# Own values first, keys and queries later, and expert tails beside the causal attention's units

## The chip, the cores and the metric

The kernel runs on one core of one Trainium2 chip, which is called trn2 below. The metric is the device time of one execution in microseconds (us). The times given are the median of three runs, with the lowest and the highest; the profile is of one execution of its own, whose time stands beside it.

## The reference

2048 tokens of width 128 go through a chain of layers, each added to the stream `x`. The first layers (a feed-forward, an attention, a feed-forward, and a mixture of experts on either side of a long convolution) are not touched. What follows is:

```python
# L2: half a feed-forward, rotary attention over all tokens, half a feed-forward
x = x + 0.5 * swiglu(norm(x))
x = x + attention(rope(norm(x) @ Wq), rope(norm(x) @ Wk), norm(x) @ Wv) @ Wo   # 16 heads of 8
x = x + 0.5 * swiglu(norm(x))
# then twice a gated block, with a causal rotary attention between the two
def gated_block(x):
    rows = norm(x)
    q = rows @ q_w;  q = q * 2 * sigmoid(head_scale(q))
    ctx = attention(q, rows @ k_w, rows @ v_w)          # all tokens, 16 heads of 8
    rows = rows + (sigmoid(ctx @ gate_w + gate_b) * ctx) @ out_w
    rows = norm(rows) * n1_g + n1_b
    out = rows + weight * (rows + res_scale * expert(rows))   # one of 8 experts for each token, by the router
    return x + 0.5 * (norm(out) * n2_g + n2_b)
x = gated_block(x)
x = x + causal_attention(rope(...)) @ Wo                # L3: as L2's, with a causal mask
x = gated_block(x)
```

(This is cut and written in short; the widths, the norms and the order are those of the reference.) All of it is float32.

## The kernel before, in words

**Tiles and units.** The tokens are cut into four chunks (`NC` = 4) of 512 (`CW`), each of four tiles of 128 (`TC` = 4). The 16 heads form four groups (`NG`) of four. A unit of an attention is (query chunk, group). For each unit two passes are made: a score pass (`sn` on TensorE, and `h_mx` on VectorE for the maximum of each row), and a weight pass (`st` on TensorE, `pr` = exp on ScalarE, `av` on TensorE). Between the passes the maxima are transposed (`mt_ps`), cast (`h_mT`) and written as extra rows into the query tile by four small DMAs (`qp<-h_mT`). At the end of a unit it is normalised (`close`), and after the fourth group of a chunk the projection is added to the stream (`finish`).

**The loop.** `attend` runs steps n = 0, 1, 2, and so on. A step takes one weight piece of the unit under way and one score piece of the unit that comes one or two later, each in two halves, so that TensorE, VectorE and ScalarE overlap. While no weights have been computed the mode is "fill"; then it is "core"; and once the scores of this call are done, the scores of the next call (`after`) begin, in mode "drain". What runs outside of the loops has mode "free", and "host" is the mode of the earlier mixture of experts, which has chunk tasks of the first call as its guests. The attention calls are, in order: `rope2` (L2), `gated[0]`, `rope3` (L3, causal), `gated[1]`.

**Guests.** Chunk tasks are Python generators, and each `yield` gives the number of ticks after which the task goes on. The list `beside` holds the chains of tasks; `guests()` advances the first two of it, twice for each step in "fill" and once elsewhere. Among them are `prepare(c)` (norm, transpose, keys of chunk c, and for chunk 0 its query), `value(c)` (the values into `va`), `query(c)`, `l2_chunk(c)` (half a feed-forward) and `route(c)` (the router). `carried` is what the previous call has left over. At L1135, L1136 and L1137 it is set that the carried chains come first, then the chunk's own values, and that `asking` holds the queries of chunks 1 to 3, which start as soon as the first unit is scored.

**Order on the engines.** Instructions of the loop are pinned: each engine keeps the order in which the program issues them. TensorE is in order, so an instruction that waits holds up all that stands behind it. The loads have their queues: most are issued by SyncE (`SP`), the rotary tables (`cos`, `sin`, L883) by GpSimd (`POOL`) outside of "free".

**Keys and queries.** In "fill" the keys of a chunk are spread on the chip (`keys_here`, L793): projection `pj`, rotation `rot`, then for each group two `spread` products and two evictions into `kp`. In the other modes `send` writes them to DRAM (`dk`), and `load_keys` reads them back into `kp`, half by half, in four loads of 128 KB for each half; where they wait in `waiting_keys`, the next call issues these loads at its beginning. Queries go to DRAM too (`dq`), and `begin` reads a unit's back into a `qp` tile.

**Rows of ones.** `head_buffers` has a function `rows`, which fills `qp`, the extra rows of `kp` (in whole columns of 128 partitions) and `va` at the start of the first call: half 0 on VectorE and ScalarE, half 1 later on GpSimd. L1564, L1572, L1576 and L1579 are these fills.

**Norms.** `norm` (L196) takes statistics on VectorE, then an inverse square root in small instructions (L185 to L188), which are on GpSimd in the modes "host" and "fill" and otherwise on VectorE, and normalises on ScalarE (L213).

**Experts.** `Experts.run` (L1325) computes the products for the slots of the experts, and then gathers each chunk's results by indirect DMAs (L1500) into `yg`. `tail(c)` weights and adds them, norms the sum and adds it to the stream. After `experts[0]`, the tails and `rope3.prepare(c)` of chunks 0 to 2 are run to their end one after another, outside of a loop, and the fourth chunk's go as a carried chain into the causal call:

```python
            for c in range(NC - 1):
                finish_all([tail(c), *after(c)])
            return [chain([tail(NC - 1), *after(NC - 1)])]
```

Of the kernel before, what the change touches and what calls it, by code (L numbers as in the profile page):

```python
# [21 lines left out]
P = 128  # L22
# [8 lines left out]
HD = 8  # L31
# [12 lines left out]
def tile_macaron(ctx: ExitStack, tc: tile.TileContext, a: dict, out: bass.AP):  # L44
# [151 lines left out]
    def norm(src, dst, on_act=False):  # L196
        stats = small.tile([P, TC, 6], F32, tag="ln_stats", name="ln_stats")
        mv = small.tile([P, TC, 2], F32, tag="ln_mv", name="ln_mv")
        for t in range(TC):
            vec.bn_stats(stats[:, t, :], src[:, t, :])  # L200
            vec.bn_aggr(mv[:, t, :], stats[:, t, :])
        on_pool = on_act and order["mode"] in ("host", "fill")
        rstd = inv_sqrt(small, mv[:, :, 1], [P, TC], "ln", on_pool)
# [514 lines left out]
    def four(ps):  # L718
        return ps.rearrange("p (t d) -> p t d", d=D)
# [48 lines left out]
    class Heads:  # L768
# [23 lines left out]
        def keys_here(self, c):  # L792
# [3 lines left out]
            for g in (0, 1, 3, PARK):  # L796
# [8 lines left out]
                self.loaded.add((c, g))  # L805
                yield 1

        def send(self, which, c):
# [9 lines left out]
            if which == "q":  # L818
                self.sent.add(c)
            elif order["mode"] == "drain":  # L820
                self.load_keys(c, (0,))
                self.waiting_keys.append((c, (1,)))
            else:
                self.waiting_keys.append((c, (0, 1)))
# [34 lines left out]

        def query(self, c):  # L860
            yield from self.send("q", c)

# [9 lines left out]
    class RopeHeads(Heads):  # L872
# [18 lines left out]
        def project(self, which, c, hi, lo):  # L891
            tables = list(self.tables(c))
            cols = self.wp[self.pre + "_bcol"]
            n = 0 if which == "q" else 2
# [83 lines left out]
    def attend(A, carried, follow, after=None):  # L978
# [156 lines left out]
        own = chain([A.value(c) for c in range(NC)])  # L1135
        asking = [chain([A.query(c) for c in range(1, NC)])]  # L1136
        beside += [[0, task] for task in (*carried[len(beside):], own)]  # L1137
        followed = 0
# [14 lines left out]
        while nw < len(weights) or last:  # L1153
# [14 lines left out]
            if s and B is not A and units[0] not in B.queries:  # L1168
                if 0 in B.sent:
                    begin(B, units[0])  # L1170
                else:
                    s = None
            if s and s[1] not in B.queries:
                s = None
# [67 lines left out]
    class Experts:  # L1242
# [82 lines left out]
        def run(self, carried, after):  # L1325
# [170 lines left out]
            for c in range(NC):  # L1496
                results.append(four(wide_tile("yg")[:, 0:CW]))
                for t in range(TC):
                    i = c * TC + t
                    nc.gpsimd.indirect_dma_start(  # L1500
                        results[c][:, t, :], None, og[:, :],
                        bass.IndirectOffsetOnAxis(ap=slot_i[:, i : i + 1], axis=0),
                    )

            def tail(c):
                yg = results[c]
                y = self.heads.rows[c]
                for t in range(TC):
# [3 lines left out]
                    )  # L1512
                norm(y, y, on_act=True)
                vec.tensor_tensor(y, y, bc(w["b3_n2g"], TC), ALU.mult)
                vec.tensor_tensor(tiles_of(x, c), tiles_of(x, c), y, ALU.add)
                yield 2

            for c in range(NC - 1):
                finish_all([tail(c), *after(c)])
            return [chain([tail(NC - 1), *after(NC - 1)])]  # L1520

# [32 lines left out]
    def head_buffers(pool):  # L1554
# [6 lines left out]
        def rows(half):  # L1561
# [6 lines left out]
            for p in range(4 * half, 4 * half + 4):  # L1568
                dst = kp[:, p, 0:n].rearrange("p (t d) -> p t d", d=P)
                src = ones.unsqueeze(1).to_broadcast([P, n // P, P])  # L1570
                if p < 2:
                    nc.scalar.activation(dst, src, AF.Identity, bias=one_rows, scale=0.0)  # L1572
                else:
                    engine = nc.gpsimd if half else nc.vector
                    tc.keep_in_program_order(
                        engine.tensor_scalar(dst, src, 0.0, one_rows, ALU.mult, ALU.add)  # L1576
                    )
            if half == 0:
                tc.keep_in_program_order(nc.gpsimd.memset(va_flat, 1.0))  # L1579

# [44 lines left out]
    carried = attend(gated[0], carried, lambda c: [experts[0].route(c)])  # L1625
    carried = experts[0].run(carried, lambda c: [rope3.prepare(c)])
    carried = attend(rope3, carried, lambda c: [gated[1].prepare(c)], gated[1])
# [110 lines left out]
```

## Time and profile before

| what | value |
| --- | --- |
| median of 3 runs | 4072.75 us (4072.22 to 4075.01) |
| profiled execution | 4067.55 us, span 4065.8 us |
| granted TensorE clock over the span | 0.886 |
| TensorE busy | 3587.3 us (88%) |
| VectorE busy | 3124.2 us (77%) |
| ScalarE busy | 2377.6 us (58%) |
| GpSimd busy | 293.5 us (7%) |

The stages, by the times of their first and last instructions in the trace (us from the start of the span): the layers up to the experts of L1 to 742, with the first chunk tasks of L2 as guests from 490; `rope2` 742 to 1557; `gated[0]` to 2370; the experts' products to 2486, with gathers from 2488; tails and keys of three chunks to 2556; `rope3` to 3124; `gated[1]` to 3905; the second experts, tails and store to 4066.

How to read it: PE is TensorE, PEld its weight loads, DVE VectorE, ACT ScalarE, POOL GpSimd, SP SyncE, and a q behind the name means its queue. The page has the span in 40 slices of 101.6 us with the busy tenths of each engine and the granted clock (PEclk). The table of windows gives the busy time of each engine in a stretch, with the number of instructions. The chain of waits follows the work that ended last back from step to step; its pieces named "issue" are time in which the engine waited for nothing that the profile shows. A mean over the span mixes stages with different limits.

### The profile page before, as it was taken

Reading aid. Unit: us, or ns where it says so; the run is one execution under the profiler, and the core shown is the slowest. Engines: PE = TensorE matmul, PEld = TensorE weight load, DVE = VectorE, ACT = ScalarE, POOL = GpSimd, SP = SyncE. Lnnn points to the kernel's source line nnn. Section 1 sums busy time; section 2 is a strip of 40 time slices with the busy share of each in tenths; the row PEclk is TensorE's granted clock in tenths of the full one; section 3 lists DMA queues with packets and bytes.
Section 4 is the critical chain, followed back from the end, with each engine's and each line's share of the span. In section 5 each row is a group of like instructions: output and inputs, shape, how many; then the busy total and the mean of one; then the engine's idle time right before and its main releaser. Section 6 shows DMA issues by size and latency. Waiting matters only on the chain.

```text
span 4065.8 us, 72224 instructions
## 1 busy us (share of the span) xinstructions
PE 3587.3 (88%) x29160; PEld 1706.7 (42%) x29160; DVE 3124.2 (77%) x5433; ACT 2377.6 (58%) x4513; POOL 293.5 (7%) x557
## 2 busy tenths in 40 slices
PE   8779899689999996899999965689997899999965
PEld 8656655333333343333333343343333333333333
DVE  2855344569999984799999844699996799999844
ACT  1222133158888873688888722256675588888732
POOL 2100011220000000000000023200000000000013
PEclk8889799879999997899999966588898799999965
DMA  2100001120000002100000022400002100000012
GB/s 65 31 1 1 1 8 34 45 61 7 10 8 8 7 2 53 35 7 10 7 10 5 7 62 78 109 15 10 10 2 63 40 9 7 10 7 7 7 51 66
DMA packets 63695, 98.97 MB, mean 24 GB/s; under 512 B 9104, under 2 KB 29312, under 8 KB 63104
## 3 DMA queue, kind: packets, MB, share of 16 engines
q1 hardware_dynamic: 53200, 69.22, 6.2%
q0 software_dynamic: 8816, 24.55, 2.5%
q8 instruction: 230, 3.77, 0.4%
q14 instruction: 105, 0.86, 0.1%
q10 hardware_dynamic: 1344, 0.57, 0.1%
HBM read 64.25 MB, written 29.00 MB: 23 GB/s over the span
## 4 chain that ended last, share of the span: by engine, by line
PE 76%; DVE 12%; ACT 4%; issue 3%; POOL 2%; DMA 2%; SPq 0%; POOLq 0%; ACTq 0%; DVEq 0%
PE av L76 23%; PE st L76 18%; PE sn L1006 10%; PE po L76 5%; PE h L76 5%; DVE h_mx L84 4%; ACT pr L1063 2%; PE ph L76 2%; DVE st L84 1%; PE km L76 1%; PE gu L76 1%; PE ot_ps L94 1%; PE mt_ps L94 1%; PE kv L76 1%; DVE ln_stats L84 1%
## 5 line engine op out<-in xcount | busy, mean ns | idle before, releaser
L84 DVE TENSOR_REDUCE h_mx<-sn 128x2 f32<-128x1024 f32 (+1 forms) x1856 | 2206.1, 1197 | 142.4 <-PE sn L1006 120.0
L1063 ACT ACTIVATE pr<-st 128x512 f32<-128x512 f32 x3712 | 1972.8, 585 | 510.5 <-PE st L76 331.7
L76 PE MATMUL av<-pr,va 128*32 128x256 f32 x14592 | 1187.1, 397 | 11.1 <-ACT h_ot L1092 11.1
L76 PE MATMUL st<-qp,kp 64*128 64x512 f32 x3712 | 998.2, 499 | 48.2 <-ACT pr L1063 45.9
L1006 PE MATMUL sn<-kp,qp 64*128 64x512 f32 (+3 forms) x3712 | 811.8, 415 | 122.0 <-DVE h_mx L84 49.0
L76 PEld LDWEIGHTS st<-qp,kp 64*128 64x128 f32 x3712 | 393.7, 187 | 821.5 <-ACT pr L1063 442.4
L76 PEld LDWEIGHTS av<-pr,va 128*32 128x32 f32 x14592 | 292.6, 109 | 663.1 <-issue 625.8
L1006 PEld LDWEIGHTS sn<-kp,qp 64*128 64x128 f32 x3712 | 387.5, 195 | 177.0 <-issue 64.2
L614 ACT ACTIVATE hid<-h 128x512 f32<-128x512 f32 x128 | 76.3, 597 | 232.5 <-PE h L76 226.9
L84 DVE TENSOR_TENSOR hid<-hid,h 128x512 f32<-128x512 f32 x128 | 87.3, 687 | 112.6 <-PE h L76 100.6
L76 PEld LDWEIGHTS po<-w_l_w3T,hid 128*128 128x128 f32 x1024 | 126.6, 194 | 39.0 <-issue 27.7
L76 PE MATMUL po<-w_l_w3T,hid 128*128 128x128 f32 x1024 | 128.7, 278 | 5.4 <-DVE hid L84 5.3
L1420 POOL DMA_INDIRECT wt<-in_b_wt,w_row_i x30 | 28.7, 958 | 1429.1 <-DVE slot_i L84 1384.5
L76 PE MATMUL h<-m_xc,w_l_w12T 128*128 128x512 f32 x256 | 126.8, 633 | 0.1
L76 PE MATMUL h<-xnT,w_l_w12T 128*128 128x512 f32 x256 | 117.4, 601 | 0.4 <-DVE logits L594 0.4
L247 POOL TENSOR_TENSOR x<-x,w_b_n2b 128x512 f32<-128x512 f32 x8 | 10.1, 1265 | 1126.3 <-DVE rows L84 1121.0
L84 DVE BATCH_NORM_STATS2 st<-ph 128x6 f32<-128x256 f32 x46 | 19.9, 432 | 89.7 <-PE ph L76 89.7
L1035 ACT CAST h_mT<-mt_ps 8x512 fp32r<-8x512 f32 x64 | 36.9, 576 | 67.9 <-PE mt_ps L94 67.7
L84 DVE TENSOR_TENSOR st<-st,mask_kq 128x128 f32<-128x128 f32 x256 | 63.2, 290 | 14.1 <-PE st L76 13.3
L76 PEld LDWEIGHTS h<-m_xc,w_l_w12T 128*128 128x128 f32 x256 | 49.6, 204 | 50.6 <-issue 47.3
L213 ACT ACTIVATE xn_t<-x,ln_nb,ln_r 128x128 f32<-128x128 f32 x52 | 21.4, 482 | 79.7 <-POOL ln_nb L208 67.9
L94 PE MATMUL xn_tp<-ident,xn_t 128*128 128x128 f32 x64 | 20.8, 406 | 52.6 <-ACT xn_t L213 49.1
(422 smaller groups left out, 2923.7 us busy)
## 6 DMA issues: line engine op xcount, KB each, us to landing
qp<-dq SPq DMA_DIRECT2D x128, 136.0 KB
kp<-dk SPq DMA_DIRECT2D x76, 128.0 KB
dq<-hi SPq DMA_DIRECT2D x32, 256.0 KB
dq<-lo SPq DMA_DIRECT2D x32, 256.0 KB
wt<-in_b_wt SPq DMA_DIRECT2D x16, 258.0 KB
qp<-h_mT SPq DMA_DIRECT2D x240, 4.0 KB
cos<-in_l_cos POOLq DMA_DIRECT2D x12, 256.0 KB, 4.1
sin<-in_l_sin POOLq DMA_DIRECT2D x12, 256.0 KB, 5.2
```

The costliest lines, as they stand in the source:

```text
L76: pin(nc.tensor.matmul(dst, lhsT=lhsT, rhs=rhs, start=start, stop=stop))
L84: ins = method(*args, **kw)
L94: pin(nc.tensor.transpose(dst, src, ident))
L213: nc.scalar.activation(dst[:, t, :], src[:, t, :], AF.Identity, bias=nb[:, t : t + 1], scale=rstd[:, t : t + 1])
L247: nc.gpsimd.tensor_tensor(xs, xs, row.unsqueeze(1).to_broadcast([P, TC, D]), ALU.add)
L614: nc.scalar.activation(hid[:, hb, :], p_1, AF.Silu)
L1006: pin(nc.tensor.matmul(sc[:, j, :wd], lhsT=qp[r, p, t * P : (t + 1) * P], rhs=kp[r, 2 * g + p, kc * CW : kc * CW + wd], start=True, stop=True,
L1035: nc.scalar.copy(mT, pt)
L1063: nc.scalar.activation(pr[:, off:CW], sc[:, off:], AF.Exp, scale=A.scale)
L1420: nc.gpsimd.indirect_dma_start(wts[k], None, a["b3_wt"], bass.IndirectOffsetOnAxis(ap=w_row_i[:, s - E : s - E + 1], axis=0),)
```

## The change

It has these parts:

1. `norm` uses GpSimd for the inverse square root only in "host", so in "fill" it is on VectorE.
2. `keys_here` in a call that is not causal stops after group 0, until the first unit has been scored, and spreads the other three groups then.
3. `send` in "free" and "core" issues the key loads at once instead of keeping them in `waiting_keys`.
4. `query` in a call that is not causal waits 12 ticks first.
5. `project` of the rotary heads in "core" waits 4 ticks between the loads of its tables and its products.
6. In `attend`, a causal call has no `asking` of its own, and its own values come ahead of the carried chains. If a score's query isn't there but has been sent, `begin` is called for it. In `rope2` no score is issued before tick 6.
7. `Experts.run` gathers into a ring of four buffers (tag "xnT") and not into the wide tiles. Only chunk 0 is finished serially; the others are three carried chains. A tail yields between its norm and its product.
8. After `experts[0]`, chunks 1 to 3 have their query behind their keys in the same chain.
9. `rows` fills slices of 32 partitions, two instructions for each column set, and the fill of `va` is no longer kept in the program's order.

```diff
@@ norm
-        on_pool = on_act and order["mode"] in ("host", "fill")
+        on_pool = on_act and order["mode"] == "host"
@@ Heads.keys_here
                 self.loaded.add((c, g))
                 yield 1
+                while g == 0 and not self.causal and self.scored < self.first:
+                    yield 1
@@ Heads.send
             if which == "q":
                 self.sent.add(c)
+            elif order["mode"] in ("free", "core"):
+                self.load_keys(c)
             elif order["mode"] == "drain":
@@ Heads.query
+            if not self.causal:
+                yield 12
             yield from self.send("q", c)
@@ RopeHeads.project
             tables = list(self.tables(c))
+            if order["mode"] == "core":
+                yield 4
@@ attend
-        asking = [chain([A.query(c) for c in range(1, NC)])]
-        beside += [[0, task] for task in (*carried[len(beside):], own)]
+
+        asking = [] if causal else [chain([A.query(c) for c in range(1, NC)])]
+        carried = carried[len(beside):]
+        beside += [[0, task] for task in ((own, *carried) if causal else (*carried, own))]
@@ attend, the loop
-            if s and s[1] not in B.queries:
+            if s and B is A and s[1] not in queries and s[1][0] in A.sent:
+                begin(A, s[1])
+            if s and (s[1] not in B.queries or A is rope2 and tick < 6):
                 s = None
@@ Experts.run
-                results.append(four(wide_tile("yg")[:, 0:CW]))
+                results.append(four(ring("yg", "xnT", (P, CW), 4)))
@@ tail
                 norm(y, y, on_act=True)
+                yield 2
                 vec.tensor_tensor(y, y, bc(w["b3_n2g"], TC), ALU.mult)
@@ Experts.run
-            for c in range(NC - 1):
-                finish_all([tail(c), *after(c)])
-            return [chain([tail(NC - 1), *after(NC - 1)])]
+            finish_all([tail(0), *after(0)])
+            return [chain([tail(c), *after(c)]) for c in range(1, NC)]
@@ rows
             for p in range(4 * half, 4 * half + 4):
-                dst = kp[:, p, 0:n].rearrange("p (t d) -> p t d", d=P)
-                src = ones.unsqueeze(1).to_broadcast([P, n // P, P])
-                if p < 2:
-                    nc.scalar.activation(dst, src, AF.Identity, bias=one_rows, scale=0.0)
-                else:
-                    engine = nc.gpsimd if half else nc.vector
-                    tc.keep_in_program_order(
-                        engine.tensor_scalar(dst, src, 0.0, one_rows, ALU.mult, ALU.add)
-                    )
+                for j in range(2):
+                    r = slice(j * KD + 4 * HD, (j + 1) * KD)
+                    dst = kp[r, p, 0:n].rearrange("p (t d) -> p t d", d=P)
+                    src = ones[r, :].unsqueeze(1).to_broadcast([4 * HD, n // P, P])
+                    if p < 2:
+                        nc.scalar.activation(dst, src, AF.Identity, bias=one_rows[r, :], scale=0.0)
+                    else:
+                        engine = nc.gpsimd if half else nc.vector
+                        tc.keep_in_program_order(
+                            engine.tensor_scalar(dst, src, 0.0, one_rows[r, :], ALU.mult, ALU.add)
+                        )
             if half == 0:
-                tc.keep_in_program_order(nc.gpsimd.memset(va_flat, 1.0))
+                nc.gpsimd.memset(va_flat, 1.0)
@@ the calls
-    carried = experts[0].run(carried, lambda c: [rope3.prepare(c)])
+    carried = experts[0].run(carried, lambda c: [rope3.prepare(c)] + [rope3.query(c)] * (c > 0))
```

## The prediction

> **What bounds the kernel now.** I read the page's slices first, then the table of windows over the stages, then the chain of waits where a window is poor, then the timeline for durations.
>
> The slices show where TensorE is far from full:
>
> ```profile
> PE   8779899689999996899999965689997899999965
> DVE  2855344569999984799999844699996799999844
> PEclk8889799879999997899999966588898799999965
> ```
>
> Each slice is 101.6 us. The attention calls are the runs of nines (slices 8 to 14, 16 to 22, 25 to 37); between them lie dips at 740 to 880 (first call starts), 1480 to 1690 (gated call starts), 2380 to 2690 (experts, causal call starts), 3080 to 3220 (second gated call starts). The change acts in the dips. The windows (PE, PEld, DVE, ACT, POOL busy, then granted clock, DMA share, GB/s):
>
> ```profile
> 742.00:770.00 28.00, 7.49 (x38) 5.51 (x38) 11.15 (x25) 5.31 (x7) 8.89 (x17) 0.62 0.52 100
> 800.00:830.00 30.00, 22.81 (x60) 10.78 (x59) 17.94 (x17) 6.72 (x11) 4.86 (x5) 0.61 0.06 18
> 830.00:880.00 50.00, 33.41 (x156) 11.72 (x154) 25.78 (x29) 16.65 (x29) 22.83 (x29) 0.70 0.43 95
> 880.00:1300.00 420.00, 417.63 (x4008) 159.18 (x4004) 408.66 (x388) 362.25 (x673) 1.27 (x1) 1.00 0.03 11
> 2486.00:2556.00 70.00, 21.30 (x39) 9.43 (x40) 35.21 (x153) 13.80 (x31) 29.05 (x27) 0.57 0.31 86
> 2556.00:2602.00 46.00, 28.89 (x83) 15.41 (x83) 26.29 (x60) 9.90 (x19) 16.84 (x42) 0.57 0.50 110
> 2800.00:2900.00 100.00, 93.32 (x804) 38.41 (x796) 93.16 (x152) 69.00 (x141) 0.00 (x0) 0.91 0.03 8
> ```
>
> In a steady call PE is at 99% and full clock (2.57 us for each step of the loop). In the starts PE works a quarter to three quarters of the time, at a clock of 0.57 to 0.70. And the body of the causal call (2800 to 2900) has DVE at 93%: a guest task put there isn't free. The chain of waits through the first call's start (start, us, what):
>
> ```profile
> 752.02 13.05 DMA kp<-dk
> 765.31 1.70 PE sn L1006 x4
> ...
> 814.15 2.00 PE spread L76 x4
> ...
> 872.44 5.16 DMA sin<-in_l_sin
> ```
>
> The first score waits 13 us for keys; four spreads and a rotation stand between scores; then the entry into the core waits for a sine table of chunk 1's query. Through the start of the first gated call and of the causal one:
>
> ```profile
> 1598.79 0.50 ACT rows L213
> ```
>
> ```profile
> 2533.23 4.34 issue
> ...
> 2546.30 7.23 issue
> ...
> 2578.39 7.33 issue
> ```
>
> In the gated start the chain passes a norm that waits for POOL. In the causal start it is an engine's own queue (POOL's and SP's DMAs), three chunks' tails, norms and keys one after another.
>
> **The change part by part.** The sum is made against the profiled execution (4067.55 us, span 4065.8); that is 5.2 us under the median of 4072.75, so I add 5.2 at the end.
>
> **1. First call's start (742 to 883).** Rows of kp are now filled only in 32-partition slices: two instructions for one, so DVE 2 x 0.97 becomes 4 (+1.9 us), ACT 2 x 1.52 becomes 4 (+3.0), POOL 4 x 1.53 becomes 8 (+6.1, after the first units, when POOL is idle). I cost these at nothing: the 13 us wait covers DVE's and ACT's part, nothing near reads POOL's half; without the cover they would cost 5. In exchange the key loads share no partition with the fills and need not wait for them: the 12 loads that began at 751.65 on SP can begin after the 2.49 us fill of qp, near 748 (SP then also issues qp's loads behind it). That is -4. Against it, the 12 late loads on POOL, which stood after the first scores, are no longer held by the fill and go out at the head of the call.
>
> Here two rows of the timeline bear on it:
>
> ```profile
> 750.38 0.85 POOL L186 TENSOR_TENSOR ln_h<-ln_h,ln_v 128x4 f32<-128x4 f32 x1
> ...
> 752.15 0.20 POOL L186 TENSOR_TENSOR ln_h<-ln_h,ln_v 128x4 f32<-128x4 f32 x1
> ```
>
> The same POOL instruction takes 0.85 us while DVE fills kp and 0.20 us after. The Trainium skill ("SBUF — State Buffer", section "SBUF: two separate sides") explains such a row: DVE and GpSimd share a port pair under an exclusive lock. Norms moved to DVE escape it; POOL's loads come later than its row suggests. A rule that speaks against the hoist is in "DMA: Bandwidth & Descriptors", "Issuing engines are not separate DMA queues": loads from POOL and SP interleave on the same 16 engines. The trace has 12 loads at a DMA share of 0.52. By the rule alone, twice the bytes could make 13.05 us into 26: the first score at 774 instead of 765.3 (+9). By the row, half the engines' time is free and POOL issues after its 2.45 us memset: -4. I take -3 and keep -8 to +9.
>
> Values of chunks 0 to 3, transposes and the first feed-forward product are now put ahead of the first score on PE (three empty steps): about 7 us of PE work that stood between scores (767.0 to 775.2) is done inside the 13 us wait: -5. Keys of chunk 3 spread one group first, three later: three spread pairs leave the stretch 811 to 822 (4 x 1.5 us with PE waiting for ACT): -4.5; they come back in steps 17 to 20, hidden behind scores at +2. The norm goes from POOL (14 instructions, 0.28 us apart: 4 us) to DVE (12, 0.20 apart: 2.4 us): -1.5. The query of chunk 1 leaves the entry into the core: there 6.5 steps took 842 to 883 = 41 us, and 6.5 x 2.57 = 16.7 at the steady pace: -24. It comes back later, with three rotations at full clock and without a wait, at +9; and the core's entry still warms the clock and loads ACT's table: +5. Sum: -3 -5 -4.5 +2 -1.5 -24 +9 +5 = **-22** (-5 to -35).
>
> **2. First gated call's start.** Norms on DVE: the chain waits there at 1588 to 1599 and 1630 to 1637, 18 us; POOL's 14 against DVE's 12 is 1.6 each and the queue ahead of POOL (bias add, rotation, 1.3 each) the rest: 2 x 3 saved. Spreads deferred: three pairs as above, -5. The query (q_ps 1.1, sg_ps 1.1, tanh 0.6, full 0.7 and its casts) and values leave the start, -7; the same work in the core, where PE is at 99%, costs its PE and wait time back, with the late spreads: +10. **-8** (-16 to +3).
>
> **3. Second gated call.** One norm and the same moves, with less carried: **-4** (-8 to +3).
>
> **4. Causal call.** Only chunk 0's tail, norm and keys stay serial. Before: gathers to 2507, then tails and keys of chunks 0, 1, 2 to 2556 with 49 us of DVE at half load. After: chunk 0 alone, with its query's landing (3.8 + 8.5 us) behind it: first score near 2541, **-15** (-5 to -25). The fill from there to the first weights, 46 us before, no longer has 16 key loads (2561 to 2574.5) ahead of the query loads on SP, nor chunk 3's tail, keys and query; 16 steps' worth of score and mask work at the rate of this window gives 31: **-15** (-8 to -22). Next comes what is late: chunk 1's query follows its keys. The projection is at step 14, sent at 15 and wanted at 16: pj 3.8, rot 1.5, POOL 1.3, ACT 0.7, POOL 1.3, issue 1.8, landing 3.8, then qp 8.5, 23 us, of which 10 pass in steps 14 and 15: PE, which runs in order, stands 13; beside this tail 2 is +6 and the rotations of chunks 2 and 3, which had been here, are -9: **+10** (0 to +20). At step 35 eight key loads of chunk 2 (0.85 us each on SP) stand ahead of the four small qp<-h_mT rows that a weight waits for: **+6** (0 to +7). Then chunks 2 and 3: each has 4 rows (1.8), two norms' statistics (3.7), 24 small instructions (4.8), multiply and add (1.4), rotations (1.5), 13 us of DVE; in a body with DVE at 93% the two cost 26, less what falls into its 7% and PE's idle 7%: **+18** (+5 to +30). Sum **+4** (-40 to +30).
>
> **5. End.** The last experts finish in the same order, covered by nothing and changed by nothing: 0 (-1 to +2). The gathers' new buffers hold nothing that is still read by then: 0.
>
> Total -22 -8 -4 +4 = -30: profiled 4037.5, median 4042.7, called 4042.
>
> **The rivals.**
> *The causal start's idle really goes.* From 2486 to 2690 DVE is idle 71 us of 204 and PE 80. If guests fill gaps that I count as full (the body's 7% over 390 us holds 27) and the query comes in time, the +10, +6 and +18 shrink to +5 together: 4042 - 29 = about 4013; with a larger start, 4005. For it: PE's idle in the body. Against: PE's order is fixed, and a guest's wait is PE's wait.
> *Slower.* One mechanism: PE's fixed order in the causal body. A moved chunk has three handovers where PE stands until DVE, ACT, POOL or a DMA has done (transposes, projection, query landing). If each chunk's query arrives as late as chunk 1's, that is 3 x 13 = 39, with SP's 6 and DVE's 26 in full 71, against the 30 saved ahead: the causal call loses 41. With 34 won elsewhere the net is +7; with the key loads at the bad end (+9 for -3) it is +19: 4092. It decides when the causal body grows by more than 64 us beyond its start's 30.
> *No change.* Loads bound the first start at the rule's +9, and the core's entry keeps its 24 because the queries, 12 ticks later, meet the same table wait: -22 becomes about +10; with -12 and +4 the sum is near 0: 4073.
>
> **How the numbers follow.** My forecast 0.50 (own range 4020 to 4060), larger gain 0.20, no change 0.12, slower 0.18. About 0.2% (8 us) is what a measurement of this kernel can tell from no change. Of the forecast's half nearly all is faster by more; faster 0.70, same 0.12, slower 0.18. The range cuts half of the slower case and the far end of the larger gain: 4008 to 4080.
>
> **What would show it.** First sn after the l1 feed-forward near 762 and the core entered (first stretch with PE at full clock) some 22 us earlier; no sine wait ahead of it; no POOL ln_h in the starts but L0's; first causal score near 2541; sn of unit (1,0) with an idle time of some 13 us released by qp<-dq; kp<-dk x8 ahead of qp<-h_mT on SP in the causal body; DVE over 95% there. It is wrong if the first score comes after 770, if the causal call ends later than 20 us after before's distance from the gathers, or if no score waits for qp<-dq.

## The result, and the profile after

The changed kernel is slower: median 4085.61 us (4077.06 to 4091.41, 6 runs) against 4073.88 us for the kernel before (4068.86 to 4078.24, 6 runs). The ratio is 1.0027, with an interval of 1.0014 to 1.004. That is +11.7 us where -30 was forecast. The profiled execution took 4077.06 us (span 4075.2), 9.5 us more than before's; it is the fastest of the six.

The page's slices of the changed kernel, to be laid beside those of before:

```profile
PE   8789899699999996999999864678997999999965
...
DVE  2855344599999975899999744688996799999844
...
PEclk9889799789999996999999955678898799999965
```

The dip after the first call's start is gone (slice 8 of PE, counted from 0, from 8 to 9), and the one around the causal call's start has got wider: the slices 22 to 27 are 8, 6, 4, 6, 7, 8 (9, 6, 5, 6, 8, 9 before). The windows of before, in the changed kernel (span, then busy PE, PEld, DVE, ACT, POOL, granted clock, DMA share, GB/s):

```profile
742.00:770.00 28.00, 12.54 (x24) 5.38 (x24) 12.03 (x21) 6.22 (x10) 8.44 (x11) 0.58 0.76 133
800.00:830.00 30.00, 20.31 (x51) 8.66 (x52) 24.32 (x26) 4.69 (x7) 2.52 (x2) 0.57 0.00 1
830.00:880.00 50.00, 48.53 (x384) 19.44 (x384) 45.27 (x42) 37.77 (x69) 18.11 (x16) 0.88 0.10 31
...
2556.00:2602.00 46.00, 40.41 (x202) 19.28 (x202) 33.59 (x86) 23.04 (x49) 2.49 (x3) 0.63 0.01 2
2690.00:2800.00 110.00, 87.12 (x613) 38.23 (x610) 91.79 (x200) 53.83 (x119) 8.41 (x9) 0.79 0.22 49
2800.00:2900.00 100.00, 93.38 (x751) 39.13 (x751) 89.40 (x139) 66.85 (x133) 2.53 (x2) 0.89 0.07 21
```

830 to 880 is now a core (384 PE instructions for 156). 742 to 770 has DMA at 0.76 (0.52 before), and fewer PE instructions (24 for 38). In the causal call the start is better filled (202 for 83 instructions in 2556 to 2602), but 2690 to 2800 is emptier: before, it was

```profile
2690.00:2800.00 110.00, 99.80 (x787) 43.46 (x784) 103.75 (x194) 64.70 (x140) 0.00 (x0) 0.89 0.04 12
```

Where it is won and lost is best seen at milestones that every unit has. A unit's milestone is the start of `h_ot`, ScalarE's copy of its finished product `av`. The table takes it from the timelines (one execution of each kernel) and says by how many us each kernel is ahead (-) of before or behind (+) it. Unit 15 is the end of the first call, 31 that of the first gated call, 32 to 47 are the causal call, 63 is the end of the second gated one. The kernels E1 to E14 come below.

| unit | before, us | changed | E1 causal undone | E2 causal alone | E5 two serial | E7 pieces | E14 pieces, two ticks |
| --- | --- | --- | --- | --- | --- | --- | --- |
| 0 | 909.05 | -25.3 | -22.7 | -1.2 | -23.0 | -26.6 | -23.4 |
| 15 | 1574.74 | -19.3 | -17.1 | -1.8 | -15.7 | -21.1 | -16.1 |
| 31 | 2351.54 | -16.1 | -16.8 | -1.6 | -15.3 | -20.6 | -15.6 |
| 33 | 2647.39 | -46.1 | -15.7 | -28.5 | -31.3 | -57.3 | -37.4 |
| 34 | 2662.44 | -27.2 | -15.5 | -9.3 | -23.1 | -44.0 | -34.9 |
| 37 | 2738.33 | -1.5 | -16.5 | +14.0 | -5.1 | -34.5 | -10.1 |
| 40 | 2831.83 | +12.2 | -12.1 | +32.1 | -1.9 | +10.9 | -2.2 |
| 43 | 2935.47 | +15.8 | -9.4 | +33.0 | -0.5 | +17.4 | -1.7 |
| 47 | 3159.09 | +10.9 | -10.0 | +32.5 | -5.0 | +16.6 | -0.5 |
| 63 | 3887.05 | +11.2 | -10.0 | +32.8 | -5.0 | +16.9 | -1.6 |

The changed kernel wins 16 us up to the causal call, wins 30 more at its start, and loses 62 between units 33 and 43. That loss is no accident of one execution: the profiles of E2, E3, E4 and E6, which have the same chunks beside the units, lose 57 to 61 us there. The stretch from unit 33 to unit 43 in the changed kernel, then before (columns as above):

```profile
2601.30:2951.28 349.98, 287.12 (x2120) 124.44 (x2120) 295.43 (x581) 185.20 (x394) 17.74 (x19) 0.81 0.14 35
```

```profile
2647.39:2935.47 288.08, 261.18 (x2080) 113.44 (x2080) 268.58 (x478) 175.09 (x371) 0.00 (x0) 0.88 0.03 11
```

PE is idle for 63 us there (27 before), and busy for 26 us more, at a granted clock of 0.81 for 0.88. VectorE has 27 us more to do, but its share of the stretch falls from 93% to 84%. The view of waits says for what PE stood (total us, times, longest; the changed kernel from 2580 to 2860 first, then before from 2600 to 2860):

```profile
PE st L76 <- ACT pr L1071: 35.7, 29, 7.5
PE sn L1014 <- DMA qp<-dq: 11.2, 2, 9.2
PE st L76 <- DMA qp<-h_mT: 4.2, 1, 4.2
...
PE mt_ps L94 <- DVE h_mt L84: 2.6, 1, 2.6
```

```profile
PE st L76 <- ACT pr L1063: 22.9, 36, 2.6
PE sn L1006 <- DVE h_mx L84: 3.4, 5, 0.8
```

Three kinds are new: a query that comes late, a row behind key loads on SyncE's queue, and waits for `pr` of up to 7.5 us. Taken over exactly the stretch of units 33 to 43, the waits for `pr` grow by 17.3 us (36.9 for 19.6), and 11.2 for the query, 4.2 for the row and 2.6 for `h_mt` are new: nearly all of the 36 us by which PE's idle time grew. The timeline at one wait for `pr` (start, duration, engine, operation):

```profile
2724.77 1.13 DVE L84 SCALAR_TENSOR_TENSOR rows<-yg,rw,rows 128x128 f32<-128x128 f32 x4
...
2729.71 0.16 DVE L84 SCALAR_TENSOR_TENSOR ln_nb<-ln_mv,ln_r 128x4 f32<-128x4 f32 x1
2729.79 0.49 DVE L84 TENSOR_TENSOR st<-st,mask_kq 128x128 f32<-128x128 f32 x2
2729.91 1.65 ACT L213 ACTIVATE rows<-rows,ln_nb,ln_r 128x128 f32<-128x128 f32 x4 [5.35 <-DVE ln_nb L84]
...
2731.46 0.58 ACT L1071 ACTIVATE pr<-st 128x128 f32<-128x128 f32 x3
2731.77 0.47 PE L76 MATMUL st<-qp,kp 64*128 64x128 f32 x1 [6.83 <-ACT pr L1071]
```

Chunk 3's tail goes out on VectorE in one burst of 5 us, sums, statistics and inverse square root; the mask of the weights stands behind it. ScalarE then does the tail's normalisation (1.65 us) ahead of the exp, and PE waits for the exp.

### The profile page after: what moved, and what is told of

Same layout as the page of the kernel before. It is cut to its first block, busy times and chain, and to the rows that moved or that the text cites. A ratio compares the mean times of both kernels' runs of the same rounds, so it can differ in the third digit from the quotient of the medians.

```text
span 4075.2 us, 72165 instructions
## 1 busy us (share of the span) xinstructions
PE 3588.6 (88%) x29160; PEld 1709.6 (42%) x29160; DVE 3137.5 (77%) x5515; ACT 2380.0 (58%) x4515; POOL 279.4 (7%) x453
## 5 line engine op out<-in xcount | busy, mean ns | idle before, releaser
L76 PE MATMUL av<-pr,va 128*32 128x256 f32 x14592 | 1192.8, 398 | 11.9 <-ACT h_ot L1100 10.8
L247 POOL TENSOR_TENSOR x<-x,w_b_n2b 128x512 f32<-128x512 f32 x8 | 10.1, 1268 | 1003.5 <-DVE rows L84 843.2
L84 DVE TENSOR_TENSOR sn<-sn,mask_qk 128x256 f32<-128x256 f32 x128 | 54.4, 425 | 26.4 <-PE sn L1014 25.8
L76 PEld LDWEIGHTS h<-xnT,w_l_w12T 128*128 128x128 f32 x256 | 47.1, 195 | 47.6 <-issue 46.4
```

The source lines that it names most:

```text
L76: pin(nc.tensor.matmul(dst, lhsT=lhsT, rhs=rhs, start=start, stop=stop))
L84: ins = method(*args, **kw)
L247: nc.gpsimd.tensor_tensor(xs, xs, row.unsqueeze(1).to_broadcast([P, TC, D]), ALU.add)
```

## The experiments

All ratios are to the kernel before in runs on the same chip, with a 95% interval. The chips were five: one for E1, E2, E5 and E6, and others for E3, E4, E7 and E8, for E9 to E12, for E13 to E15, and for E17 and E18. Across chips, kernels are compared by their ratios. The edits are cut to what matters (`...`), and against the changed kernel where nothing else is said.

**E1, the causal and expert parts undone.**

```diff
-            elif order["mode"] in ("free", "core"):
-                self.load_keys(c)
...
+        asking = [chain([A.query(c) for c in range(1, NC)])]
+        beside += [[0, task] for task in (*carried[len(beside):], own)]
...
-            finish_all([tail(0), *after(0)])
-            return [chain([tail(c), *after(c)]) for c in range(1, NC)]
+            for c in range(NC - 1):
+                finish_all([tail(c), *after(c)])
+            return [chain([tail(NC - 1), *after(NC - 1)])]
```

> The changed kernel with its causal and expert parts undone: three chunks' tails and keys are serial again ahead of the causal call, its queries are asked for as before, the key loads wait for the next call, and the gathers are in the wide tiles. Theory A (the causal body pays for the moved chunks; the milestones lose 27 us between the gathers and the end of the causal call): the 16 us won in the first two calls stay and the 27 go, so about 4058 us, 0.996 of before, and all h_ot of the causal call stand 16 us ahead of before's. Rival B (the loss is from the norms on VectorE and the key gating, which the causal call has too): it stays within 5 us of the changed kernel, 4080 to 4090. Rival C (run to run, the two kernels are alike): 4073 to 4085.

4052.73 us, 0.9956 (0.9943 to 0.9969). Theory A; rival B would have needed 4080. The causal call no longer has the -46 and the +16.

**E2, the same parts alone, on the kernel before.**

> The kernel before with only the causal and expert parts of the change (chunk 0 alone serial, the others carried with their queries, own values first, key loads at once, the wait after the tables, the ring for the gathers). Norms in the fill stay on GpSimd. Theory A: it loses what the causal call lost in the changed kernel, 25 to 30 us: about 4100 us, 1.0065 of before. Rival B (norms on VectorE): with the fill's norms on GpSimd the loss is halved, 4085 or less. Rival C: 4073.

4101.7 us, 1.0065 (1.0043 to 1.0087), the figure of theory A. The table shows the same shape as for the changed kernel, with no lead to begin with. So the parts add: the causal and expert parts cost 0.65%, the others win about 0.44%.

**E5, chunk 1 serial too.**

```diff
-            finish_all([tail(0), *after(0)])
-            return [chain([tail(c), *after(c)]) for c in range(1, NC)]
+            for c in range(2):
+                finish_all([tail(c), *after(c)])
+            return [chain([tail(c), *after(c)]) for c in range(2, NC)]
```

> The changed kernel with chunks 0 and 1 (tail, norm, keys, query) finished serially and only 2 and 3 beside the units. Theory A: chunk 1's query is there in time, so the wait of 11 us for qp<-dq at unit (1,0) goes and the fill has no tail, at the price of some 15 us of serial time; the waits of chunks 2 and 3 stay. Net -5 to +5 against the changed kernel: 4080 to 4090. Theory A' (chunk 1's late query and the burst of its successors is most of the loss): 4065 to 4072, since the chunks behind it come earlier too. Rival B: no difference but the serial time, 4095 to 4100.

4064.11 us, 0.9979 (0.9968 to 0.999): the low end of what A' has. The start gives up 15 us (unit 33) and the loss between units 33 and 43 falls from 62 to 31. No score of the body waits for qp<-dq any more, and VectorE's extra work in this stretch falls from 27 to 14 us: half the moved work there, half the loss.

**E6, the late half of the rows filled in whole columns.** The first half stays in slices; the late key loads, which write into the columns of the second half, wait for its fills again.

```diff
+            whole = half == 1
             for p in range(4 * half, 4 * half + 4):
-                for j in range(2):
-                    r = slice(j * KD + 4 * HD, (j + 1) * KD)
+                for j in range(1 if whole else 2):
+                    r = slice(0, P) if whole else slice(j * KD + 4 * HD, (j + 1) * KD)
```

> The changed kernel with the second half's rows of kp filled in whole columns on GpSimd, as before; so the 12 late key loads wait for those fills again and don't share the DMA engines with the first loads. Theory D (the shared engines hold up the second score, which waits 5.8 us for kp<-dk in the changed kernel): the second score comes at 759 to 760 instead of 765.5, and the call is 4 to 6 us shorter: 4079 to 4081. Rival E (the fill is bound by VectorE's maxima anyway): the second score is earlier and the maxima of the first unit end where they did, 829 to 831: 4084 to 4087.

4077.73 us, 1.0011 (1.0 to 1.0022), 6.5 us under the changed kernel's ratio, with intervals that overlap: theory D in size, and the trace decides for it. The first score and the one that waited, in the changed kernel and then in E6:

```profile
758.92 0.76 PE L1014 MATMUL sn<-kp,qp 64*128 64x512 f32 x1 [4.54 <-DMA qp<-dq]
...
765.51 0.76 PE L1014 MATMUL sn<-kp,qp 64*128 64x512 f32 x1 [5.82 <-DMA kp<-dk]
```

```profile
753.42 0.79 PE L1014 MATMUL sn<-kp,qp 64*128 64x512 f32 x1
...
755.77 0.76 PE L1014 MATMUL sn<-kp,qp 64*128 64x512 f32 x1 [1.55 <-DMA kp<-dk]
```

The second score comes 9.7 us earlier, and the first unit's maxima are transposed at 818.4 us, 12.8 ahead of before (1.3 in the changed kernel). The other profiles agree: all ten kernels with the early fill in slices and the late one whole have this transpose at 817.9 to 823.1 us, all seven with both in slices at 828.7 to 832.7. The DMA view of 742 to 832 in the changed kernel, and then in E6, fits (all packets, and GpSimd's queue q0 with packets, MB and share of the engines):

```profile
DMA packets 2246, 5.04 MB, mean 56 GB/s; under 512 B 433, under 2 KB 433, under 8 KB 2242
...
q0 software_dynamic: 881, 2.56, 16.0%
```

```profile
DMA packets 1899, 3.75 MB, mean 42 GB/s; under 512 B 396, under 2 KB 396, under 8 KB 1895
...
q0 software_dynamic: 535, 1.27, 4.9%
```

In E6 1.29 MB of GpSimd's loads no longer run in this stretch beside SyncE's.

**E3, the causal body's inverse square roots on GpSimd.**

```diff
-        on_pool = on_act and order["mode"] == "host"
+        on_pool = on_act and (order["mode"] == "host" or order["mode"] == "core")
```

> The changed kernel with the inverse square root of the norms in the causal body (two tails, two norms of chunks 2 and 3) on GpSimd instead of VectorE. In the changed kernel each of these norms is followed by a wait of TensorE for pr of 2.6 to 7.5 us. Theory F (VectorE's burst holds up the mask adds of the weights): 10 small instructions of 0.2 us leave VectorE four times, -8 us, 4077. Theory G (ScalarE is what is held: its normalisation stands ahead of the exps, and waits for the whole chain wherever it runs): GpSimd's chain is longer (0.28 against 0.20 us for each), so +4 to +6: 4089.

4074.94 us, 1.0014 (1.0001 to 1.0027): 5 us under the changed kernel, with overlapping intervals. The longest wait for `pr` is 3.6 us (7.5), so F's direction; G's loss did not come. But the stretch from unit 33 to unit 43 still loses 57 us (62): the longest waits are a small part of the loss.

**E4, the key loads in the causal body on GpSimd's queue.**

```diff
-                self.load_keys(c)
+                self.load_keys(c, queue=nc.gpsimd if order["mode"] == "core" else nc.sync)
```

> The changed kernel with the key loads of chunks 2 and 3 in the causal body issued by GpSimd and not by SyncE. The small rows qp<-h_mT then have nothing ahead of them on SyncE. Prediction's step (head of line, forecast 6, seen as one wait of 4.2 us for qp<-h_mT): -4 us, 4081. Rival (GpSimd's loads hold up its rotations, and those a query): 0 to +4.

4077.7 us, 1.0019 (1.0003 to 1.0034). The wait for qp<-h_mT is 0.3 us (4.2), so the head of line is shown by the wait; the gain in time, 3 us, is inside the intervals.

**E7, the norms of the causal body in pieces.**

```diff
+    def norm_steps(src, dst):
...
+        for t in range(TC):
+            vec.bn_stats(stats[:, t, :], src[:, t, :])
+            vec.bn_aggr(mv[:, t, :], stats[:, t, :])
+            if t % 2:
+                yield 1
+        rstd = inv_sqrt(small, mv[:, :, 1], [P, TC], "ln", True)
...
+        yield 3
+        for t in range(TC):
+            nc.scalar.activation(
...
+            if t % 2:
+                yield 1
@@ normed_chunk
+        if order["mode"] == "core":
+            yield from norm_steps(tiles_of(x, c), xn)
...
@@ tail
-                norm(y, y, on_act=True)
+                if order["mode"] == "core":
+                    yield 1
+                    yield from norm_steps(y, y)
+                else:
+                    norm(y, y, on_act=True)
```

> The changed kernel with the tails' and norms' work of the causal body cut into pieces with steps of the loop between them: the sums, the statistics of two tiles at a time, the inverse square root on GpSimd, three ticks, then ScalarE's normalisation two tiles at a time. The same work, only not in one burst. Theory F and G alike (a burst of a guest holds up an in-order engine, VectorE or ScalarE): the waits of 7.5, 2.6, 6.8 and 5.2 us shrink to 1 to 2 each, -15 us, 4070. Rival H (VectorE is full, so the work costs its time however it is laid): 0 to -5 us, 4080 to 4086. The chunks come some ticks later, which may cost a score's wait.

4097.84 us, 1.0066 (1.0047 to 1.0084): a miss for every theory, by its sign. Its profile is of the fastest execution, 4084.29 us. It shows two things at once: at unit 37 it is 33 us ahead of the changed kernel, and between 37 and 40 it loses 45. Part of the lead is work that is only put off: from unit 33 to unit 37 VectorE does 11 us less than in the changed kernel (89.2 for 100.5). The waits from 2580 to 2860:

```profile
PE st L76 <- ACT pr L1094: 25.2, 33, 2.2
PE sn L1037 <- DMA qp<-dq: 24.2, 4, 11.4
```

The bursts' waits are gone (longest 2.2 us; 2.6 before the change). Two of the four waits for qp<-dq are those of chunk 1's query (10.8 us, as in the changed kernel). The other two are chunk 2's query, which the pieces put off by ticks:

```profile
2754.08 0.79 PE L1037 MATMUL sn<-kp,qp 64*128 64x512 f32 x1 [11.36 <-DMA qp<-dq]
```

It costs more than this wait. The loop goes on without a score while the query hasn't been sent, so PE has weights and no scores from 2716 to 2754, and then scores and no weights from 2773 to 2802: the two passes no longer overlap.

**E14, E7 with two ticks for each step of the causal body.** The work and its pieces are the same; only the guests run twice as fast.

```diff
                 guests()
+                if causal and order["mode"] == "core":
+                    guests()
```

> The changed kernel with its causal norms in long pieces (the version that measured 1.0066) and with two ticks of the guests for each step of the causal body instead of one. Theory (a deadline: in that version the queries of chunks 2 and 3 came after the scores that want them, 24 us of waits for qp<-dq and two losses of 20 us): with two ticks they come in time, at most 10 us of waits for qp<-dq stay (chunk 1's), and the lead of 30 us at unit (1,2) is kept in part: 4060 to 4070, 0.997 to 0.999. Rival (VectorE is full, the moved work costs its time in whatever order): the lead is spent by the bursts that two ticks bring back, 4085 to 4098.

4063.4 us, 0.9976 (0.9966 to 0.9986), by the ratios 0.9% or 37 us under E7: the deadline theory. Its waits in the same stretch:

```profile
PE st L76 <- ACT pr L1094: 35.1, 37, 3.1
PE st L76 <- DMA qp<-h_mT: 5.7, 1, 5.7
PE sn L1037 <- DVE h_mx L84: 3.3, 5, 0.9
```

No score waits for a query, chunk 1's included. The waits for `pr` are back to 35 us, in smaller pieces. E14 is also 0.5% under the changed kernel, but no run has two ticks without the pieces, so how much of this the pieces give is not shown.

**E11, E17 and E18: chunks serial, pieces and ticks combined**, all with the late fill whole and shorter pieces (statistics, one tick, inverse square root on GpSimd, two ticks, ScalarE's part). E11 has two chunks serial and one tick, E17 one chunk serial and two ticks, E18 two chunks serial and two ticks. The shorter pieces, against E7's:

```diff
             vec.bn_aggr(mv[:, t, :], stats[:, t, :])
-            if t % 2:
-                yield 1
+        yield 1
         rstd = inv_sqrt(small, mv[:, :, 1], [P, TC], "ln", True)
...
-        yield 3
+        yield 2
...
-            if t % 2:
-                yield 1
```

> The changed kernel with chunks 0 and 1 serial, the late fill whole and the norms of the causal body cut into shorter pieces (statistics, a tick, the inverse square root on GpSimd, two ticks, ScalarE's part). The version with long pieces was 30 us ahead at unit (1,2) of the causal call's end and then lost 40 because the queries of chunks 2 and 3 came after the scores that want them. Here they start earlier by chunk 1's ticks and take fewer. Theory (bursts and deadlines): 4064 - 7 for the loads - 8 to -12 for the bursts = 4047, 0.9945. Rival (chunk 3's query still misses): 4060 or more, with a wait for qp<-dq of over 5 us.

> The changed kernel (chunk 0 alone serial) with two ticks for each step of the causal body, short pieces and the late fill whole. If deadlines and the first call's loads are the two causes and add: 0.9976 less 0.0016, about 4064 to 4066 against a before of 4074, 0.996; if the moved chunks could win what their serial time was (a lead of 26 us at the call's start), under 0.992; if short pieces bring bursts back, 0.998 to 1.0.

> Chunks 0 and 1 serial, short pieces, two ticks for each step of the causal body, the late fill whole. The version with one tick had 0.9953, and no wait for a query. If only a missed deadline is what costs, two ticks change nothing here: 0.995. If two ticks bring bursts closer together, 0.997.

E11 4056.31 us, 0.9953 (0.994 to 0.9966); E17 4066.4 us, 0.9981 (0.997 to 0.9993); E18 4062.14 us, 0.9969 (0.9958 to 0.998). E11 is near the 0.9945 of its theory. It is 0.26% under E5, of which the late fill gives about 0.16% (E6), so little is left for the pieces. E17 is not told apart from E14: the loads' gain is in its first maxima (823.1 us) and not in its time. Its expectation puts that down to bursts that come back, but from 2580 to 2860 its waits for `pr` are 29.3 us with 2.7 as the longest, less than E14's, so the reason stays open. In E11 and E18 alike no score of the body waits for a query, and two ticks cost 0.16%, with intervals that just overlap.

**E8 to E10, E12 and E13: what the other parts are worth**, all with the causal and expert parts undone. E8 has the late fill whole as well.

> The changed kernel with the causal and expert parts undone and the second half's rows of kp filled in whole columns: what was won in the first call and in its loads, without what was lost in the causal call. If the two effects add: 0.9956 of before less 6 to 8 us, about 4046, 0.9938. If the later start of other transfers takes the second away: 4053.

4045.19 us, 0.9941 (0.992 to 0.9962): the sum of E1's gain and E6's, though its interval overlaps E1's.

E10 is E8 without the wait ahead of the queries:

```diff
-            if not self.causal:
-                yield 12
             yield from self.send("q", c)
```

> The version with the causal parts undone and the late fill whole, without the wait of 12 ticks ahead of the queries of calls that are not causal. Prediction's step: the query in the core's entry costs 24 and later only 9, so this loses 15 in the first call, and in the gated ones about 0: 4060, 0.998. Rival (the entry's loss is the clock and the key rows, not the query): 0 to 3.

4063.67 us, 0.9981 (0.9968 to 0.9995): 0.4% or 16 us lost to E8, where the prediction's step has 15. E10's view of waits from 830 to 890 shows the wait that the changed kernel does not have:

```profile
PE sn L1010 <- DVE rot L84: 9.8, 1, 9.8
```

E9 is E8 with the fill's norms on GpSimd (the first edit), E12 is E8 with all keys spread at once (the second), and E13 is both.

```diff
-        on_pool = on_act and order["mode"] == "host"
+        on_pool = on_act and order["mode"] in ("host", "fill")
...
-                while g == 0 and not self.causal and self.scored < self.first:
-                    yield 1
```

> The version with the causal parts undone and the late fill whole (4045 us, 0.9941 of before), with the fill's norms on GpSimd again, as before. Prediction's steps: the norms on VectorE win 1.5 in the first start, 6 in the gated one and about 3 in the second, so this loses about 10: 0.9965. Rival (VectorE is the fuller engine in a fill, and in the causal call the milestones of the version without this lose 5 us at the first unit): 0 to -5, 0.993 to 0.994.

> The version with the causal parts undone and the late fill whole, with all four groups of a chunk's keys spread at once in the fill (the gating of the last three groups undone). Prediction's step: the gating wins 4.5 and gives 2 back in the first call, 5 in each gated start and gives them back in the core; so this loses 3 to 6 in all: 0.995. Rival (moved work only moves, since the core has TensorE at 99%): within 2 us, 0.994.

> The version with the causal parts undone, the late fill whole, the keys spread at once and the fill's norms on GpSimd again. Of the change only the later queries, the wait after the tables, the empty first steps and the sliced first fill stay. If the norms' move is worth nothing (rival of that experiment: 0.9931 against 0.9941), it is within 3 us of 0.9912; if it costs something, 0.990; if the move wins where keys are spread at once, 0.993.

| | norms on VectorE | norms on GpSimd |
| --- | --- | --- |
| keys gated | E8 0.9941 (0.992 to 0.9962) | E9 0.9931 (0.9917 to 0.9945) |
| keys at once | E12 0.9912 (0.9898 to 0.9927) | E13 0.9951 (0.9934 to 0.9967) |

Inconclusive: the means over rows are 0.9936 and 0.9932, those over columns 0.9927 and 0.9941. Taken over the other part, neither is worth more than about 0.2% either way. But E12 and E13 differ by 0.39%, with intervals that don't meet, while E8 and E9 are alike: where the keys are spread at once the norms on VectorE may win. E12 has four runs and E13 nine, on different chips, and E12 is not told apart from E9, so this stays open.

**E15, E11 with both of these edits.**

> Chunks 0 and 1 serial, 2 and 3 beside the causal units with norms in short pieces (0.9953 in its version with gated keys), the late fill whole, the keys spread at once and the fill's norms on GpSimd. If the gain of the keys (0.29% between the versions without the causal parts) adds: 0.992, about 4043. That beside-the-units work is then worth nothing against the serial one (0.9912) would show in the two being alike; if overlapping wins something, under 0.990.

4054.67 us, 0.995 (0.9935 to 0.9966), the same as E11's 0.9953: the gain of the keys did not add, as E13, with the same two edits, has none over E8. E15 is also the same as E13's 0.9951, which differs in that all chunks but the last are serial: chunks beside the causal units won nothing over that. The serial versions E8, E9, E12 and E13 have 0.9912 to 0.9951, the best with chunks beside the units 0.995. The lowest median is E12's, 4042.45 us.

## Why the prediction was wrong, point by point

- **First call, -22 forecast, -19.3 measured at its end.** Right in sum, by luck: two errors nearly cancel. The fill's -12 (-3, -5, -4.5, +2, -1.5) came out as -1.3. The key loads had been put at -4 by the timeline's row and at +9 by the shared DMA engines; the sum took -3, and the shared engines decided, for with the late loads out of the way (E6) the fill gave 12.8. The query's step was right in kind and too small: -24.0 between the first transposed maxima and unit 0 (-1.3 to -25.3), and 6.0 given back by the end of the call, where -24, +5 and +9 were forecast. E10 shows its 16 us.
- **First gated call, -8 forecast, +3.2 measured** (-19.3 to -16.1). Its start wins 3.6 where -6, -5 and -7 were forecast, and by unit 18 the core has taken 7 of the forecast's 10 back. So the start's terms are what failed. The two-by-two experiment gives neither the norms' 6 nor the gating's 5 a clear worth; which of the three is most wrong stays open.
- **Second gated call, -4 forecast, +0.3 measured**, in the same way: -4.5 in the start, given back within three units.
- **Causal call, +4 forecast, +27.0 measured** (-16.1 to +10.9). Its start was right: the forecast's 2556 is the second score (a lone first one stands at 2544.7), and the second score comes 53.6 us after the first gather (67.4 before), -14 for -15; the lead grows to 30 at unit 33, for -15 and -15. The wait for chunk 1's query was right, 11.2 us for 13, and SyncE's head of line too, 4.2 for 6.
- **Causal call, the body: the step that failed.** For it +10, +6 and +18 make 34; it lost 62 up to unit 43, and 57 up to the end of the call. With the two waits taken out, 47 us stand where +6, -9 and +18 were forecast. **The mis-sized term is the +18 for chunks 2 and 3.** It had the work right (26 us of VectorE; 27 measured between units 33 and 43) and its price wrong: it counted this work against the idle of the engines, as if it could be poured into gaps of a body that VectorE bounds. The work comes in bursts of about 5 us between instructions of the loop, on the way from a score to its exp, and VectorE's share fell to 84% where the list of signs has over 95%. Of the 47, some 21 are PE's idle time, most of it waits for `pr` (17.3 more). The other 26 are PE's busy time, a term that the sum put at nothing: the same stretch ran at a granted clock of 0.81 for 0.88. An estimate from these two figures: 261 us at 0.88 make 284 at 0.81, so the clock is some 23 of the 26, and the 40 added PE instructions the rest. (E10 and E12 at the end of this document bear such an estimate out: 104.8 us at 0.92 make 116 at 0.83, where 114.9 were measured.) Why the clock was lower there, and what part of the waits is due to the bursts' length alone stay open: E7 ends the long waits and loses the gain to a deadline, E3 halves the longest for about 5 us.
- **The rival "slower"** had PE's fixed order in the causal body as its mechanism, deciding when the body grows by more than 64 us. It grew by 57 to 62, and the kernel is slower by 11.7, because the other calls gave 16 us and not 34. Its price (71) was nearer than the forecast's 34. Its picture (each chunk's query 13 us late) holds for chunk 1 alone: in the changed kernel chunks 2 and 3 pay without a late query, and chunk 2's is late only in E7.
- **The other rivals.** "The causal start's idle really goes" needed +10, +6 and +18 to shrink to 5 together; they grew. "No change" was right in that the loads bound the first start, and wrong in that the entry keeps its 24: the entry lost it.
- **What would have shown it**: the list of refutations named a causal call that ends later than 20 us after before's distance from the gathers, and this came true: unit 47 comes 694.2 us after the first gather, for 670.7 (of the 27.0 above, 3.4 lie ahead of the gathers). It also named a first score after 770. That came at 758.9; the second, at 765.5 (765.8 before), was the one to watch, since the loads serve every score. One reading was loose: slices 8, 16, 25, 26, 30 and 31 of the row of TensorE before, which are counted among the runs of nines, have 8, 8, 6, 8, 7 and 8.

## What to carry to other kernels

Work that is moved from a serial stretch to the side of a loop can cost a multiple of its busy time: here a stretch with 27 us more of it on VectorE took 62 us longer. Ask two things of it: how long its longest burst is on each engine that keeps the program's order, and by when what it feeds is wanted. Cutting it into pieces mended the first here and broke the second (E7), so count ticks and pieces together (E14), and compare with leaving it serial, which was no slower. Loads that are freed from a dependency may all start at once, as here: what was kept waiting was in the better order (E6).

## What the runs showed of the hardware

The clock granted in the causal body differs between executions of the same work. The stretch from unit 36 to unit 40 has the same 862 PE instructions and nearly the same VectorE time in E10 and E12, whose program does not differ in it:

```profile
2704.21:2820.87 116.66, 104.78 (x862) 45.57 (x860) 111.98 (x201) 72.58 (x155) 0.00 (x0) 0.92 0.04 12
```

```profile
2697.80:2823.62 125.82, 114.86 (x862) 50.76 (x862) 112.22 (x200) 72.86 (x153) 0.00 (x0) 0.83 0.03 11
```

9 us more at a clock of 0.83 for 0.92, and PE busy for 10 us more. The six executions of the changed kernel go the same way, 4077.06 us at a mean clock of 0.885 and 4090.49 at 0.878. So a single profile cannot carry a difference of under 10 us in this stretch. From unit 33 to unit 43 the six kernels with the causal parts undone (E1, E8 to E10, E12, E13) lie between 1 us ahead of before and 19 us behind it, at clocks of 0.90 to 0.80, with nearly the same instructions; E8's and E12's profiles, with 12 and 19 us, are no evidence against their parts. The 57 to 62 us of the five kernels with three chunks beside the units lie well outside of this.
